# Decoder kernel, second cross attention: four engines issue in the order of the text instead of the scheduler's

## The chip, the cores and the metric

One core of a Trainium2 chip. The metric is the time of one execution in microseconds (us) of device time. The kernel before took 1747.34 us, median of three runs (1746.52, 1749.41, 1747.34). A profiled execution of it is used for everything below.

Engines by their names in the profile: PE is TensorE (matmul; PEld its weight loads), DVE is VectorE, ACT is ScalarE, POOL is GpSimd, SP is SyncE, which issues nearly all transfers. Each engine takes its own instructions strictly one after the other from its queue; semaphores order the engines among each other. L1361 means line 1361 of the kernel.

## The reference, cut to what matters

Two decoder layers over four sequences of 256 tokens, all in float32. The part that the change touches is the second layer's cross attention: 16 query heads in 4 groups that share keys and values, head size 128, and 256 + 1601 = 1857 keys for each sequence.

```python
q = (draft_hidden @ Wq.T).reshape(bsz, draft_len, H, HD)
q = _rms_norm(q, q_norm_w).transpose(0, 2, 1, 3)
kv_in = jnp.concatenate([context_hidden, draft_hidden], axis=1)
k = (kv_in @ Wk.T).reshape(bsz, total_len, KVH, HD)
v = (kv_in @ Wv.T).reshape(bsz, total_len, KVH, HD).transpose(0, 2, 1, 3)
k = _rms_norm(k, k_norm_w).transpose(0, 2, 1, 3)
q = _rope(q, draft_position_ids)
k = _rope(k, full_position_ids)
scores = jnp.einsum('bhqd,bhkd->bhqk', q, k) * SCALE
probs = jax.nn.softmax(scores, axis=-1)
attn = jnp.einsum('bhqk,bhkd->bhqd', probs, v)
return attn @ Wo.T
```

It is followed by a mixture of eight experts (`experts` in the kernel), which for one sequence is computed beside the attention of the next.

## The kernel before, in words

The kernel is written as generators that emit instructions, in a framework that records them, finds the dependencies, sets the semaphores, and lets a scheduler choose the order in which each engine gets its instructions. The first part (the first layer, and the recurrence of the second) fills about the first 500 us. The rest is `steps()` (L1531), started beside the end of the first part and then emptied by `run(work)` at L1596.

Work is done in 32 pairs of heads (4 sequences, 4 groups, 2 pairs in each). A pair has 256 tokens x 2 heads = 512 query columns and 15 tiles of 128 keys, the last of 65. Two key tiles make a chunk, so a pair has 8 chunks, the last with the 65 keys alone. One step `s` of the text emits, in this order:

- `exponential` (L1381) for the chunk scored ten steps earlier (`DE = 10`): DVE subtracts the row maximum from 128x1024 scores (L1383), ACT takes the exponential in place (L1386), POOL adds both halves to the sum (L1389 and L1398).
- `score` (L1349) for chunk `s`, twice: PE computes a 128x512 tile of scores `bsc` in PSUM in two passes (L1361); ACT copies it to SBUF with the key's norm as scale (L1362); DVE takes it into the running maximum `acc` (L1364 for the first tile of a pair, L1366 for the others).
- `others(2 s)`, then `weigh` (L1400) for the chunk of eleven steps earlier (`DW = 11`): PE multiplies the exponentials by the values into `bpo` (L1407, two tiles, four passes); then `others(2 s + 1)`.

`others` (L1524) emits what a table of places holds for that half step: `maximum` (L1368: four transposes `tm` on PE, a maximum `mq` on DVE, and a few half steps later four transposes `bc` that spread it), `finish` (L1409: `bpo` copied to `aT` on ACT, the sums `ts` turned by PE and DVE, and the output projection `bpw`, L1437, added to x on DVE, L1441), the queries of the next group (`prep_q`, L1229: `pq` on PE, squares L1189 on ACT, rotations L1190 and L1191 and a sum L1198 on DVE, an addition L1196 and a power L1199 on POOL that gives `rnq`, and later the scaling L1203 on ACT, transposes `tpq` and a copy to `qTb`), its keys in four pieces (`prep_kv`, L1258: the same with `pk`, then transposes `tpk` L1301 and the copy to `kTb` L1303), position angles and tables (L1115 to L1165), and the experts of the sequence before.

Score tiles and most other PSUM tiles go round six banks (`p1`). The scores wait in twelve SBUF chunks between `score` and `weigh`. Instructions that read the same PSUM tile on two engines are ordered by semaphores in the text's order: the copy L1362 is ahead of the maximum L1366 on the same tile, which waits for it.

The order on each engine's queue within this part was the scheduler's choice, as long as it kept the dependencies. The list `ENGINES` (L19) names PE, DVE, ACT and POOL.

The text of two of the functions named, for the order in one step:

```python
V.tensor_tensor(s[0:n, 0:w, :], s[0:n, 0:w, :], self.bc[0:n, None, :].to_broadcast([n, w, 512]), ALU.subtract)
A.activation(s[0:n, 0:w, :], s[0:n, 0:w, :], AF.Exp)
...
T.matmul(pc[0:n, :], lhsT=e["kT"][:, k * P : k * P + n], rhs=q, start=True, stop=True)
A.activation(s[0:n, i, :], pc[0:n, :], AF.Copy, scale=e["kn"][0:n, k : k + 1])
...
V.scalar_tensor_tensor(self.acc[0:n, :], pc[0:n, :], e["kn"][0:n, k : k + 1], self.acc[0:n, :], ALU.mult, ALU.max)
```

Of the kernel before, what the change touches and what calls it, by code (L numbers as in the profile page):

```python
# [12 lines left out]
ENGINES = (mybir.EngineType.PE, mybir.EngineType.DVE, mybir.EngineType.Activation, mybir.EngineType.Pool)  # L13
# [103 lines left out]
def decoder_kernel(ctx: ExitStack, tc: tile.TileContext, at, t, out):  # L117
# [988 lines left out]
    def run(gen):  # L1106
        for _ in gen:
            pass
# [422 lines left out]
    def steps():  # L1531
        for s in range(STEPS):
            n, c = divmod(s, NPAIR)
            m, i = divmod(s - DE, NPAIR)
            if 0 <= m < len(pairs):
                pairs[m].exponential(i)
            if n < len(pairs):
                pairs[n].score(c)
            others(2 * s)
            m, i = divmod(s - DW, NPAIR)  # L1540
            if 0 <= m < len(pairs):
                pairs[m].weigh(i)
            others(2 * s + 1)
            yield s
# [15 lines left out]
    work = steps()  # L1560
# [32 lines left out]
    run(late)  # L1593
    run(keys)
    run(first)
    run(work)  # L1596
    assert not places, sorted(places)
    gen = experts(B - 1)
    for _ in range(KEPT):
# [70 lines left out]
```

## Time and profile before

| | us |
|---|---|
| profiled execution | 1749.43 |
| its span, first to last instruction | 1747.4 |
| PE busy | 1694.9 (97%) |
| DVE busy | 1302.7 (75%) |
| ACT busy | 997.4 (57%) |
| POOL busy | 877.5 (50%) |

Busy time counts the time in which at least one instruction of an engine runs; instructions that follow each other overlap a little, so an instruction's own duration is longer than the distance to the next start. In the group rows the figures after the bar are busy time and mean nanoseconds of one instruction, and after the second bar the engine's idle time just ahead of them, with what ended most of it. In rows of the timeline: start, length, engine, line, operation, tiles, shapes, number of instructions merged into the row, and the idle time before it. In rows of waits: total us, how many, the longest.

### The profile page before, as it was taken

How to read it: one execution, taken by the hardware profiler on the slowest of the kernel's cores; microseconds unless marked ns; L12 is line 12 of the kernel's file. 1: busy time of each engine (PE TensorE's matmuls, PEld its weight loads, DVE VectorE, ACT ScalarE, POOL GpSimd, SP SyncE). 2: the span in 40 equal slices, each digit the busy share in tenths (PEclk: the TensorE clock that was granted, in tenths of full speed). 3: DMA queues.
4: the chain of work that ended last, by engine and by line, in shares of the span. 5: the costliest groups of instructions: out<-in, count | busy, mean ns of one | idle time of the engine just before them, and what ended most of it. 6: DMA issues, size and time to landing. Idle time of an engine off the chain costs nothing.

```text
span 1747.4 us, 20643 instructions
## 1 busy us (share of the span) xinstructions
PE 1694.9 (97%) x6642; PEld 971.5 (56%) x6642; DVE 1302.7 (75%) x2429; ACT 997.4 (57%) x1742; POOL 877.5 (50%) x719
## 2 busy tenths in 40 slices
PE   8899989999999999999999999999999999999998
PEld 4455668765555455554555555555555555445546
DVE  6653476787668777787877878777877878788776
ACT  3456653656456656566665656556565656656551
POOL 2210032211126576676766756655665776676651
PEclk9999999999999999999999999999999999999999
DMA  7221334212231121121212121121222113011102
GB/s 258 99 90 50 90 99 128 75 66 90 97 109 46 38 82 35 55 58 31 89 32 70 47 67 52 55 82 35 73 61 67 51 37 93 26 37 48 43 0 67
DMA packets 113554, 119.10 MB, mean 68 GB/s; under 512 B 10000, under 2 KB 87332, under 8 KB 113448
## 3 DMA queue, kind: packets, MB, share of 16 engines
q1 hardware_dynamic: 111624, 116.39, 21.6%
q10 hardware_dynamic: 1824, 1.41, 0.3%
q8 instruction: 53, 0.87, 0.2%
q14 instruction: 53, 0.43, 0.1%
HBM read 100.20 MB, written 17.57 MB: 67 GB/s over the span
## 4 chain that ended last, share of the span: by engine, by line
PE 64%; DVE 12%; POOL 9%; ACT 9%; issue 4%; DMA 1%; POOLq 0%; DVEq 0%; ACTq 0%
PE bpo L1407 17%; PE bsc L1361 16%; PE pk L1290 5%; POOL sum L1398 5%; PE mph L1053 2%; PE bpw L1437 2%; PE vah L355 2%; ACT s L1386 2%; ACT s L1362 2%; DVE acc L1366 1%; PE xpo L740 1%; DVE s L1383 1%; PE pq L1239 1%; POOL ropeq L1196 1%; PE xsc L695 1%
## 5 line engine op out<-in xcount | busy, mean ns | idle before, releaser
L1398 POOL TENSOR_TENSOR sum<-sum,s 128x512 f32<-128x512 f32 (+1 forms) x411 | 536.7, 1306 | 84.1 <-ACT s L1386 59.0
L1361 PE MATMUL bsc<-qTb,kTb 128*128 128x512 f32 (+1 forms) x960 | 459.5, 599 | 6.8 <-ACT kTb L1303 6.7
L1407 PE MATMUL bpo<-s,vb 128*128 128x512 f32 (+1 forms) x960 | 459.9, 598 | 0.4 <-ACT s L1386 0.4
L1362 ACT ACTIVATE s<-bsc,kn 128x512 f32<-128x512 f32 (+1 forms) x480 | 316.5, 683 | 211.6 <-PE bsc L1361 194.6
L1366 DVE SCALAR_TENSOR_TENSOR acc<-bsc,kn,acc 128x512 f32<-128x512 f32 x448 | 333.0, 743 | 89.2 <-ACT s L1362 73.3
L1383 DVE TENSOR_TENSOR s<-s,bc 128x1024 f32<-128x1024 f32 (+1 forms) x256 | 289.4, 1142 | 14.7 <-PE bc L1379 14.5
L1386 ACT ACTIVATE s<-s 128x1024 f32<-128x1024 f32 (+1 forms) x256 | 256.5, 1006 | 53.8 <-DVE s L1383 52.2
L1361 PEld LDWEIGHTS bsc<-qTb,kTb 128*128 128x128 f32 (+1 forms) x960 | 174.2, 188 | 191.9 <-issue 135.3
L1407 PEld LDWEIGHTS bpo<-s,vb 128*128 128x128 f32 (+1 forms) x960 | 169.8, 191 | 141.7 <-issue 137.9
L1389 POOL TENSOR_TENSOR sum<-s 128x512 f32<-128x512 f32 x32 | 40.8, 1276 | 198.6 <-ACT s L1386 198.6
L1196 POOL TENSOR_TENSOR ropek<-ropek,ropuk 128x512 f32<-128x512 f32 (+1 forms) x64 | 78.2, 1222 | 123.7 <-DVE ropuk L1191 122.4
L1203 ACT ACTIVATE ropeq<-ropeq,rnq 128x128 f32<-128x128 f32 x128 | 41.2, 390 | 110.7 <-POOL rnq L1199 107.1
L355 PE MATMUL vah<-wv,vcT 128*128 128x512 f32 (+1 forms) x156 | 77.7, 633 | 5.1 <-DMA vcT<-in_ctxT 3.1
L1290 PEld LDWEIGHTS pk<-wkv,cTk 128*128 128x128 f32 x624 | 76.3, 192 | 8.3 <-issue 4.5
L1290 PE MATMUL pk<-wkv,cTk 128*128 128x128 f32 x624 | 77.4, 275 | 0.0
L1199 POOL TENSOR_TENSOR kn<-ssk,nhalf 128x4 f32<-128x4 f32 (+1 forms) x64 | 66.2, 1034 | 17.5 <-DVE ssk L1198 15.0
L1364 DVE TENSOR_SCALAR acc<-bsc,kn 128x512 f32<-128x512 f32 x32 | 24.0, 750 | 59.7 <-ACT s L1362 59.7
L1437 PEld LDWEIGHTS bpw<-wo,aT 128*128 128x128 f32 x256 | 48.5, 190 | 34.8 <-issue 21.1
L272 POOL TENSOR_TENSOR rsr_xa<-rse_xa,nhalf 128x2 f32<-128x2 f32 x4 | 3.4, 854 | 126.0 <-DVE rse_xa L270 126.0
L1437 PE MATMUL bpw<-wo,aT 128*128 128x256 f32 x256 | 65.6, 379 | 0.3 <-ACT aT L1413 0.3
L1196 POOL TENSOR_TENSOR ropeq<-ropeq,ropuq 128x512 f32<-128x512 f32 x32 | 43.8, 1368 | 40.2 <-PE bsc L1361 17.8
L358 ACT COPY vst<-vah 128x512 f32<-128x512 f32 (+1 forms) x52 | 30.2, 591 | 56.0 <-issue 18.3
(509 smaller groups left out, 2589.7 us busy)
## 6 DMA issues: line engine op xcount, KB each, us to landing
v<-vst SPq DMA_DIRECT2D x48, 256.0 KB
vb<-v SPq DMA_DIRECT2D x48, 256.0 KB
cTk<-in_ctxT SPq DMA_DIRECT2D x24, 512.0 KB
wq<-in_wq SPq DMA_DIRECT2D x16, 512.0 KB
wo<-in_wo SPq DMA_DIRECT2D x16, 512.0 KB
wi<-in_wi SPq DMA_DIRECT2D x32, 256.0 KB
xcT<-in_ctxT SPq DMA_DIRECT2D x12, 512.0 KB
xct<-in_ctx SPq DMA_DIRECT2D x12, 512.0 KB
```

The costliest lines, as they stand in the source:

```text
L355: T.matmul(pv[0:r, :], lhsT=cT[:, c, k * P : k * P + r], rhs=wv[c], start=c == 0, stop=c == 1)
L1196: G.tensor_tensor(r4, r4, u4[:, :, ::-1, :], ALU.add)
L1199: G.tensor_tensor(rn, ss[:, 0:n], nhalf[:, 0:n], ALU.pow)
L1290: T.matmul(pk[:, q, 0:w], lhsT=src, rhs=e["wkv"][:, c, 0:w], start=c == 0, stop=c == 1)
L1361: T.matmul(pc[0:n, :], lhsT=e["kT"][:, k * P : k * P + n], rhs=q, start=True, stop=True)
L1362: A.activation(s[0:n, i, :], pc[0:n, :], AF.Copy, scale=e["kn"][0:n, k : k + 1])
L1366: V.scalar_tensor_tensor(self.acc[0:n, :], pc[0:n, :], e["kn"][0:n, k : k + 1], self.acc[0:n, :], ALU.mult, ALU.max)
L1383: V.tensor_tensor(s[0:n, 0:w, :], s[0:n, 0:w, :], self.bc[0:n, None, :].to_broadcast([n, w, 512]), ALU.subtract)
L1386: A.activation(s[0:n, 0:w, :], s[0:n, 0:w, :], AF.Exp)
L1398: G.tensor_tensor(self.sum[0:n, :], self.sum[0:n, :], s[0:n, i, :], ALU.add)
L1407: T.matmul(self.po, lhsT=e["v"][0:n, k, :], rhs=self.s[c][0:n, i, :], start=k == 0, stop=k == NCH - 1)
L1437: T.matmul(pw[:, j * 256 : j * 256 + 256], lhsT=aT[:, o : o + P], rhs=e["wo"][:, self.h + h, :], start=True, stop=True)
```

## The change

The call that empties `steps()` is put into a region of the framework. Within it each of the four engines gets its instructions in the order in which the text emits them; the order across engines, SP's order, and where the region stands among instructions outside it stay with the scheduler. Steps 0 to 6 are emitted before the region, and the last sequence's experts after it.

```diff
@@ -1593,7 +1593,8 @@
     run(late)
     run(keys)
     run(first)
-    run(work)
+    with tc.manual_schedule(engines=set(ENGINES)):
+        run(work)
     assert not places, sorted(places)
     gen = experts(B - 1)
     for _ in range(KEPT):
```

## The prediction

> **What bounds the kernel now.** I read the page first: the chain that ended last, then the costliest groups.
>
> ```profile
> PE 64%; DVE 12%; POOL 9%; ACT 9%; issue 4%; DMA 1%; POOLq 0%; DVEq 0%; ACTq 0%
> ...
> L1361 PE MATMUL bsc<-qTb,kTb 128*128 128x512 f32 (+1 forms) x960 | 459.5, 599 | 6.8 <-ACT kTb L1303 6.7
> L1407 PE MATMUL bpo<-s,vb 128*128 128x512 f32 (+1 forms) x960 | 459.9, 598 | 0.4 <-ACT s L1386 0.4
> L1362 ACT ACTIVATE s<-bsc,kn 128x512 f32<-128x512 f32 (+1 forms) x480 | 316.5, 683 | 211.6 <-PE bsc L1361 194.6
> L1366 DVE SCALAR_TENSOR_TENSOR acc<-bsc,kn,acc 128x512 f32<-128x512 f32 x448 | 333.0, 743 | 89.2 <-ACT s L1362 73.3
> ```
>
> Most of the chain is PE, and the other engines wait for it. Two scores of PE (L1361) feed two readers each: ACT's copy (L1362) and DVE's running maximum (L1366). The last row shows what the change will act on: DVE's maximum waits for ACT's copy, although both only read the same PSUM tile. The program's waits agree: each L1366 waits for ACT and, through acc, for the DVE instruction before it.
>
> Next the stage itself, from the first pair's last score to the last pair's (531.4 to 1684.7 us: 31 pairs of heads, 37.2 us each), and DVE's waits in it.
>
> ```profile
> core 0: us, PE busy (x) PEld busy (x) DVE busy (x) ACT busy (x) POOL busy (x), PEclk, DMA share, GB/s
> 531.40:1684.70 1153.30, 1133.75 (x4016) 612.31 (x4015) 922.68 (x1498) 698.48 (x1152) 764.40 (x614) 1.00 0.18 53
> ```
>
> ```profile
> DVE acc L1366 <- ACT s L1362: 68.8, 62, 4.3
> DVE acc L1364 <- ACT s L1362: 59.1, 26, 5.2
> ```
>
> PE is busy 98% of it. DVE is busy 922.7 us and stands 230.6. That is the room in which a worse order of DVE is free; past it, each microsecond of standing lengthens the kernel.
>
> **The change.** No instruction of the computation is added or removed. From step 7 on, four engines take the text's order. Comparing the two builds: PE's order hardly differs (a pass or two of L1407, or two scores, at each of the 15 head changes, and a little at both ends), DVE's goes backwards against the text at 355 places before and at none after, ACT's at 255, POOL's at 89. SP stays with the scheduler: some 11 of its 203 transfers change place (positions, rawk, wo, one we), with DMA 18% busy in the stage and a stage that gets longer around them; I take 0.
>
> The text of one step says, per engine: DVE subtracts (L1383, an old pair), then L1366, L1366, then whatever else; ACT takes the exponential (L1386) of that same subtraction, then copy, copy (L1362). Before, the scheduler issued subtractions ahead of the maxima, 8.7 places early on average. Now a circle closes in every step: subtraction, exponential behind it, copy behind the exponential, maximum behind the copy, next step's subtraction behind the maxima. DVE stands while ACT takes the exponential and the first copy, and nothing of its queue may pass. Behind it in that queue are both maxima, which free PSUM, and the rotations of the next keys; PE waits for those, with a step in hand.
>
> The price of one round, from rows of the timeline (DVE, then ACT, then a pair of maxima in a row):
>
> ```profile
> 881.92 0.75 DVE L1366 SCALAR_TENSOR_TENSOR acc<-bsc,kn,acc 128x512 f32<-128x512 f32 x1 [4.24 <-ACT s L1362]
> ...
> 883.90 1.19 DVE L1383 TENSOR_TENSOR s<-s,bc 128x1024 f32<-128x1024 f32 x1
> 885.00 0.75 DVE L1366 SCALAR_TENSOR_TENSOR acc<-bsc,kn,acc 128x512 f32<-128x512 f32 x1
> 885.67 1.21 DVE L1383 TENSOR_TENSOR s<-s,bc 128x1024 f32<-128x1024 f32 x1
> ```
>
> ```profile
> 880.28 1.04 ACT L1386 ACTIVATE s<-s 128x1024 f32<-128x1024 f32 x1
> 881.22 1.24 ACT L1362 ACTIVATE s<-bsc,kn 128x512 f32<-128x512 f32 x2
> ...
> 885.12 1.06 ACT L1386 ACTIVATE s<-s 128x1024 f32<-128x1024 f32 x1 [0.25 <-DVE s L1383]
> ```
>
> ```profile
> 889.46 1.61 DVE L1366 SCALAR_TENSOR_TENSOR acc<-bsc,kn,acc 128x512 f32<-128x512 f32 x2 [0.54 <-issue]
> ```
>
> Subtraction 1.20; the exponential starts 0.03 after its end (885.09 to 885.12); the copy starts 0.94 after the exponential (880.28 to 881.22) and takes 0.67; the maximum starts 0.03 after the copy's end (881.89 to 881.92); the second starts 0.86 after the first (1.61 less 0.75), for it needs acc; the next instruction follows 0.67 later. Sum 4.40. The same three DVE instructions in a row cost 1.11 + 0.67 + 0.67 = 2.45 (starts at 883.90, 885.00, 885.67). So a full step adds 1.95 us of standing. Of eight steps, one subtracts 65 rows (0.68 for 1.20, an exponential of 0.53 for 0.94): 3.47 against 1.92, adds 1.55. One scores 65 rows, once: 3.54 against 1.78, adds 1.76. A pair: 6 x 1.95 + 1.55 + 1.76 = 15.0 us.
>
> All other DVE work (rotations L1190/L1191, L1198, mq, updates of x, experts, tables) stands in the text after the second maximum and before the next subtraction: it lies beside ACT's copies, not in the standing time, so it adds in full. In the stage DVE is then busy 922.7, stands 15.0 x 30.75 = 461 (steps 10 to 255, where a score and an exponential meet), and gets some 7 us of angle rows (L1131 to L1140) that the scheduler had put ahead of 531. ACT's table loads (1.28 each) with three activations of 1.0 to 1.1 stand between a copy and an exponential at three places; some 2.4 us of each overhang: 7. Sum 1398 for 1153.3: +244. What DVE must wait for besides is there a step early: PE needs only the exponential of the step before, and its work (some 4.6 us a step by the spacing of its starts, all else included) is under the new 5.6 (1398 over 248 steps).
>
> What improves is then covered. ACT waits 104.3 us for POOL's rnq (L1203 from L1199), and PE stands four times some 2.4 us behind that or its like (at 751.8, 1059.8, 1374.7, 1547.4); text order puts L1203 behind the copies. And at head changes PE loses its filler: tpk at 857.23, a pass of L1407 at 857.66, kTb copied from 857.87, the score at 858.53; without the pass 0.87 us x 15 = 13 us. Both lie beside the DVE circle and cost or bring nothing while it binds; if that cover is gone they are the rival below. The tail after 1684.7 has no scores: unchanged, 0 (between -3 and +5).
>
> Outside the stage nothing is taken: 1747.4 + 244 = 1991, and the profiled execution lasted 2.0 us more than its span (1749.43), 2.1 above the median. I take 1994. Low end: other DVE work counted as 922.7 less all busy time of L1383, L1366 and L1364 (280.5 + 322.5 + 23.3) is 296, though their rows overlap their neighbours by 0.07 to 0.09; with the circle's bare 33.4 a pair (8 x 4.40 less 0.93 and 0.86) over 30.75 pairs this gives 1027 + 296 + 14 for the stage, 1933 in all. High end: PE standing long enough to lose its clock, below, in part: +60, 2055.
>
> A rule beside this: PE's clock. After PE stood 2.26, 2.45 and 2.34 us (751.84, 1059.79, 1547.38) the granted clock was 0.5 for 3.41 us; after 2.15 us (1374.70) it was not. [...] By the row a step with rotations of keys (4.4 + 1.9 against PE's 4.3) comes near it, one to three a pair: up to 5 us of a pair's 8 us spare. [...]
>
> **Rivals.** A, PE remains the bound: the standing fits into DVE's 230.6 us because maxima need not follow copies, or ACT is further ahead than the text says. It decides where a pair's circle with its other work stays below 37.2 us; I get 45. For it: PE's 98%, and PE's order all but unchanged. Against: the two rows of DVE waiting for ACT. Time: the four stands (9.2), kTb late for the fourth chunk (some 7) and late expert rows (3) go, 13 come: 6 less, 1743 against the execution's 1749.43, faster than before. 5%.
>
> B, PE's half clock feeds back: longer stands, slower PE, so that PE sets the pace. One half-clock window a step costs 8 x 1.7 on 36.7 us of work (PE's passes at their back-to-back spacing, 1137 us for 31 pairs), 50.3 a pair: 31 x 13.1 more, 2155. For it: stands near 2.2 us in steps with keys. Against: a slower PE stands less. 8%.
>
> C, half of the other DVE work slips into the standing time (about 120 us less), as where the exponential is ready early: 1870. Against: the built order has nothing between subtraction and maximum. That the order is not taken at all, I exclude: it is in the build. 5%.
>
> **How the numbers follow.** Forecast 82%, A 5, B 8, C 5. Its own range is 1933 to 2055; 1925 to 2075 leaves out A, B and C and little else. A measurement of this kernel tells about 0.2% (3.5 us) from no change: faster 0.04 (most of A), same 0.02, slower 0.94.
>
> **What would show it.** DVE's waits L1366 <- ACT s L1362 grow from 62 to over 400, some 1.7 us each; ACT's exponential waits for DVE's subtraction in nearly every step; L1383 and L1386 alternate step by step; pairs of 44 to 46 us; PE busy near 80%; L1203 no longer waits for rnq. It is wrong if DVE's maxima run while an exponential of the same step is still on ACT, or if PE stays over 95% busy.

## The result, and the profile after

The changed kernel takes 2008.22 us, median of four runs (2007.57 to 2012.01), against 1747.90 us (1746.52 to 1749.41) for the kernel before on the same chip: a ratio of 1.1494, 95% interval [1.1474, 1.1514]. The predicted 1994 lies 14 us below it. The profiled execution lasted 2007.57 us, its span 2005.8. All further rows of the changed kernel are of that execution.

The chain that ended last, and the four groups that were shown of before, now read on the page of the changed kernel:

```profile
PE 36%; DVE 34%; ACT 15%; issue 12%; DMA 1%; POOL 1%; DVEq 0%; ACTq 0%; SPq 0%; POOLq 0%
...
L1366 DVE SCALAR_TENSOR_TENSOR acc<-bsc,kn,acc 128x512 f32<-128x512 f32 x448 | 336.0, 750 | 391.5 <-ACT s L1362 366.7
...
L1361 PE MATMUL bsc<-qTb,kTb 128*128 128x512 f32 (+1 forms) x960 | 485.9, 626 | 115.4 <-ACT kTb L1303 99.9
L1407 PE MATMUL bpo<-s,vb 128*128 128x512 f32 (+1 forms) x960 | 475.5, 616 | 37.3 <-ACT s L1386 30.4
...
L1362 ACT ACTIVATE s<-bsc,kn 128x512 f32<-128x512 f32 (+1 forms) x480 | 301.5, 673 | 7.3 <-PE bsc L1361 7.2
```

The chain went from 64% PE to 36% PE, 34% DVE and 15% ACT. The instructions themselves hardly change on DVE and ACT (mean 750 ns for 743, 673 for 683). What is new is the idle time of DVE's maximum behind ACT's copy: 366.7 us for 73.3. ACT's copy, in turn, no longer waits for PE: 7.2 us for 194.6. PE has become the engine that is ahead.

The waits of the changed kernel:

```profile
ACT s L1386 <- DVE s L1383: 678.5, 246, 5.4
...
DVE acc L1366 <- ACT s L1362: 366.7, 219, 4.8
...
PE bsc L1361 <- ACT kTb L1303: 99.9, 49, 4.6
...
DVE acc L1364 <- ACT s L1362: 51.6, 31, 1.7
```

Before, the first of these rows read:

```profile
ACT s L1386 <- DVE s L1383: 52.2, 68, 2.6
```

246 of 256 exponentials wait for their subtraction, where 68 did, and the two kinds of maximum together wait 250 times, once in nearly every one of the 256 steps that score. 366.7 + 51.6 = 418.3 us over 250 is 1.67 us each.

One whole turn of the circle, from the timeline of the changed kernel, DVE first, then ACT over the same time:

```profile
1018.41 1.21 DVE L1383 TENSOR_TENSOR s<-s,bc 128x1024 f32<-128x1024 f32 x1
1021.32 1.61 DVE L1366 SCALAR_TENSOR_TENSOR acc<-bsc,kn,acc 128x512 f32<-128x512 f32 x2 [1.70 <-ACT s L1362]
1022.84 0.41 DVE L1059 SCALAR_TENSOR_TENSOR it<-it,mph 128x256 f32<-128x256 f32 x1
1023.29 0.42 DVE L1060 TENSOR_TENSOR it<-it,mph 128x256 f32<-128x256 f32 x1
1023.62 1.22 DVE L1383 TENSOR_TENSOR s<-s,bc 128x1024 f32<-128x1024 f32 x1
```

```profile
1019.65 1.06 ACT L1386 ACTIVATE s<-s 128x1024 f32<-128x1024 f32 x1 [4.37 <-DVE s L1383]
1020.61 1.25 ACT L1362 ACTIVATE s<-bsc,kn 128x512 f32<-128x512 f32 x2
```

Subtraction, exponential, copy, maxima, subtraction: 1023.62 - 1018.41 = 5.21 us, of which two expert rows take 0.78 (1022.84 to 1023.62). 4.43 remain, where 4.40 were predicted. This turn is no exception: each of the stage's 244 subtractions is followed on DVE by a maximum at once, and the idle time between the two is 1.70 us in the median, and nearly everywhere (1.27 where 65 rows are subtracted). The reader is to see two things: that DVE has nothing to do between 1019.62 and 1021.32, and that ACT has nothing before 1019.65. Each engine is idle while the other works.

By stretches of time (from the first pair's last score to the last pair's, and the rest):

```profile
core 0: us, PE busy (x) PEld busy (x) DVE busy (x) ACT busy (x) POOL busy (x), PEclk, DMA share, GB/s
528.60:1928.80 1400.20, 1200.34 (x4016) 624.35 (x4015) 943.54 (x1505) 685.67 (x1151) 749.24 (x611) 0.96 0.14 43
1928.80:2005.80 77.00, 61.65 (x243) 40.41 (x241) 45.97 (x107) 20.49 (x32) 22.25 (x18) 0.96 0.12 38
```

The stage lasts 1400.2 us (1153.3 before; 1398 predicted), 45.2 a pair. DVE stands 1400.2 - 943.5 = 456.7 us in it (230.6 before). The tail lasts 77.0 us, where 62.7 were left unchanged in the prediction: that is nearly the whole miss. The same row of the kernel before:

```profile
1684.70:1747.40 62.70, 56.89 (x243) 39.67 (x241) 41.86 (x99) 15.88 (x26) 17.80 (x14) 1.00 0.15 46
```

### The profile page after: what moved, and what is told of

The parts are those of the page before. It is cut to its first block, busy times and chain, and to the rows that moved or that the text cites. A ratio compares the mean times of both kernels' runs of the same rounds, so it can differ in the third digit from the quotient of the medians.

```text
span 2005.8 us, 20665 instructions
## 1 busy us (share of the span) xinstructions
PE 1765.7 (88%) x6642; PEld 984.1 (49%) x6642; DVE 1321.1 (66%) x2429; ACT 985.1 (49%) x1743; POOL 865.3 (43%) x719
## 4 chain that ended last, share of the span: by engine, by line
PE 36%; DVE 34%; ACT 15%; issue 12%; DMA 1%; POOL 1%; DVEq 0%; ACTq 0%; SPq 0%; POOLq 0%
DVE s L1383 10%; DVE acc L1366 10%; ACT s L1362 9%; PE bsc L1361 6%; PE bpo L1407 5%; PE vah L355 3%; PE pq L1239 2%; DVE x L1441 1%; DVE ropuk L1191 1%; PE mph L1053 1%; PE pp L822 1%; PE pk L1290 1%; PE xpo L740 1%; PE xsc L695 1%; DVE ssk L1198 1%
## 5 line engine op out<-in xcount | busy, mean ns | idle before, releaser
L1398 POOL TENSOR_TENSOR sum<-sum,s 128x512 f32<-128x512 f32 (+1 forms) x411 | 529.3, 1288 | 455.6 <-ACT s L1386 422.0
L1366 DVE SCALAR_TENSOR_TENSOR acc<-bsc,kn,acc 128x512 f32<-128x512 f32 x448 | 336.0, 750 | 391.5 <-ACT s L1362 366.7
L1361 PE MATMUL bsc<-qTb,kTb 128*128 128x512 f32 (+1 forms) x960 | 485.9, 626 | 115.4 <-ACT kTb L1303 99.9
L1407 PE MATMUL bpo<-s,vb 128*128 128x512 f32 (+1 forms) x960 | 475.5, 616 | 37.3 <-ACT s L1386 30.4
L1362 ACT ACTIVATE s<-bsc,kn 128x512 f32<-128x512 f32 (+1 forms) x480 | 301.5, 673 | 7.3 <-PE bsc L1361 7.2
L1407 PEld LDWEIGHTS bpo<-s,vb 128*128 128x128 f32 (+1 forms) x960 | 174.2, 197 | 197.4 <-issue 133.5
L1389 POOL TENSOR_TENSOR sum<-s 128x512 f32<-128x512 f32 x32 | 40.7, 1273 | 71.7 <-ACT s L1386 71.7
L1199 POOL TENSOR_TENSOR kn<-ssk,nhalf 128x4 f32<-128x4 f32 (+1 forms) x64 | 63.5, 992 | 17.4 <-DVE ssk L1198 14.8
L1053 PE MATMUL mph<-yTm,wi 128*128 128x256 f32 x256 | 61.8, 386 | 0.0
L1239 PE MATMUL pq<-wq,yTb 128*128 128x512 f32 x128 | 60.3, 593 | 0.0
L1441 DVE SCALAR_TENSOR_TENSOR x<-bpw,rs,x 128x256 f32<-128x256 f32 x128 | 55.3, 472 | 5.3 <-PE bpw L1437 5.3
L1364 DVE TENSOR_SCALAR acc<-bsc,kn 128x512 f32<-128x512 f32 x32 | 24.0, 751 | 51.6 <-ACT s L1362 51.6
```

Source lines behind the costliest of these rows:

```text
L1239: T.matmul(pq, lhsT=d["yT"][:, c, j * P : (j + 1) * P], rhs=e["wq"][:, c, :], start=c == 0, stop=c == 1)
L1398: G.tensor_tensor(self.sum[0:n, :], self.sum[0:n, :], s[0:n, i, :], ALU.add)
L1407: T.matmul(self.po, lhsT=e["v"][0:n, k, :], rhs=self.s[c][0:n, i, :], start=k == 0, stop=k == NCH - 1)
```

## The experiments

Theory: the loss is the circle of DVE and ACT, closed because both take the text's order. Rivals: PE's order (the filler gone at the head changes), one of the two queues alone, and a collapse of PE's clock. (On the last: the granted clock is 0.5 for 99 us of the stage, which can cost PE at most about half of that, an estimate, while PE stands 1400.2 - 1200.3 = 199.9 us besides. It does not set the pace.) All times below are medians with the kernel before timed on the same chip (1747.22, 1749.54 and 1746.34 us for the three groups of runs), and ratios are to that.

### Which engines' order

Six kernels differ from the changed one in the list of engines alone:

```diff
-    with tc.manual_schedule(engines=set(ENGINES)):
+    with tc.manual_schedule(engines={mybir.EngineType.PE}):                                     # e1
+    with tc.manual_schedule(engines={mybir.EngineType.DVE}):                                    # e2
+    with tc.manual_schedule(engines={mybir.EngineType.Activation}):                             # e3
+    with tc.manual_schedule(engines={mybir.EngineType.DVE, mybir.EngineType.Activation}):       # e4
+    with tc.manual_schedule(engines={mybir.EngineType.Activation, mybir.EngineType.Pool}):      # e10
+    with tc.manual_schedule(engines={mybir.EngineType.Activation, mybir.EngineType.PE}):        # e11
```

PE alone:

> Only TensorE takes the text's order; VectorE, ACT and POOL stay with the scheduler. Theory (the circle subtraction, exponential, copy, maximum makes the loss): the circle is not there, since the scheduler still puts subtractions ahead. What is left is the filler lost at 15 head changes, 0.87 us each: 1748 to 1765 us. Rival (TensorE's order makes the loss, its waits for kTb are 99.9 us of the changed kernel): at least 1840.

VectorE alone:

> Only VectorE takes the text's order. Theory: the circle needs both queues, and on ACT the scheduler now puts a step's copies ahead of its exponential, so the maxima find their copies done: 1745 to 1800 us. Rival (text order on VectorE alone makes the loss, because its subtractions come late): 1950 to 2010.

ScalarE alone:

> Only ACT takes the text's order. Theory: VectorE's subtractions still run ahead, so an exponential seldom waits and the circle is open: 1740 to 1800 us. Rival (ACT's order alone makes the loss, copies held up behind exponentials): 1950 to 2010.

VectorE and ScalarE:

> VectorE and ACT take the text's order, TensorE and POOL stay with the scheduler, which can fill TensorE's waits as it likes. Theory: the whole circle is there: 1985 to 2015 us, some 1.7 us of VectorE standing in each of about 219 steps. Rival (TensorE's order and its waits for kTb carry a good part of the loss): below 1930.

ACT with one of the two engines that are not in the circle:

> ACT and POOL in text order, PE and DVE left to the scheduler. ACT alone gave 1733.0. POOL's queue has the sums of the exponentials and the rotations' sums for the norm rnq; on no run so far does a row show that POOL's order binds. Theory (only a circle of two engines that both take the text's order costs much, and it takes DVE and ACT): POOL's order is covered, 1728 to 1742. Rival: POOL closes a second circle with ACT, since the sum waits for the exponential and ACT's scaling of the queries waits for rnq behind that sum: 1745 to 1775, and the wait of L1203 for rnq is back.

> ACT and PE in text order, DVE and POOL left to the scheduler. PE alone cost 14 us (the filler at the head changes is gone), ACT alone gained 14 us. Theory 1, the two are separate and add: 1744 to 1752. Theory 2, ACT's order already gives the key copies early enough that PE needs no filler: 1729 to 1739. Rival of both, ACT and PE close a circle of their own through copy, PSUM bank and score: over 1765.

| text order on | us | ratio, 95% interval |
|---|---|---|
| PE (e1) | 1762.03 | 1.0082 [1.0066, 1.0097] |
| DVE (e2) | 1766.33 | 1.0107 [1.0090, 1.0125] |
| ACT (e3) | 1732.96 | 0.9913 [0.9899, 0.9928] |
| DVE and ACT (e4) | 1997.66 | 1.1428 [1.1411, 1.1445] |
| ACT and POOL (e10) | 1729.86 | 0.9892 [0.9873, 0.9911] |
| ACT and PE (e11) | 1744.56 | 0.9985 [0.9976, 0.9994] |

DVE alone costs 19 us, ACT alone brings 14, and the two together cost 250. That is no sum of two prices: the loss needs both, as a circle does. The waits of the run with both:

```profile
ACT s L1386 <- DVE s L1383: 678.5, 247, 6.7
...
DVE acc L1366 <- ACT s L1362: 367.2, 219, 4.9
...
PE bpo L1407 <- ACT s L1386: 143.1, 100, 4.2
...
PE bsc L1361 <- ACT kTb L1303: 4.3, 9, 0.5
```

The first two rows are those of the changed kernel to within 0.5 us. PE's waits are quite others (its order is the scheduler's here): it stands 143 us for exponentials and 4 for keys, instead of 30 and 100. The time hardly notices, 1998 for 2008: PE's and POOL's text order add at most some 10 of the 260 us to what DVE's and ACT's make. So PE's stands in the changed kernel lie nearly all beside the circle, as the prediction had them.

With one of the two queues left free, the circle is open. With ACT's order free (e2), ACT copies ahead of the exponential: in one step of its timeline two copies start at 1002.59, the subtraction on DVE at 1003.13, the maxima at 1004.26 without a wait, and the exponential only at 1004.62. With DVE's order free (e3), the subtraction has been issued ahead, and ACT waits for subtractions in 39 places (102.6 us), not 246.

e3 came out below its range, and below the kernel before. Two rows of ACT's waits, first of the kernel before, then of e3, say what went:

```profile
ACT ropeq L1203 <- POOL rnq L1199: 107.1, 31, 6.5
```

```profile
ACT ropeq L1203 <- POOL rnq L1199: 3.6, 5, 1.6
```

The scheduler had put the scaling of the queries (L1203) where ACT stood for a norm still under way on POOL; the text has it behind the copies. In the stage PE's idle time falls from 19.6 us (1153.30 - 1133.75) to 6.1 (1132.60 - 1126.53), its busy time by 7.2 more, and the mean granted clock of the run is 0.996, where it was 0.993. This is the gain that the prediction priced inside rival A (19 us, of which 9 for these stands) and held to be covered.

PE's text order costs 15 us alone (e1), and 12.5 on top of ACT's (e11 is 1.8 below its own runs of before, e3 14.3): close to the 13 that rows of one head change gave. e11 fits the theory of two separate prices. In e10 the further gain over e3 (ratio 0.9892 for 0.9913) is inside the intervals, so POOL's order is worth nothing that these runs can tell; e3 and e10 both beat the kernel before and the changed one. e10's 1729.86 us is the lowest median of all these kernels; against the kernel before it is a gain of 1.1%.

### Opening the circle at one point

The maximum ahead of the copy, for the changed kernel (e5) and for the kernel before (e8):

```diff
-                A.activation(s[0:n, i, :], pc[0:n, :], AF.Copy, scale=e["kn"][0:n, k : k + 1])
                 if k == 0:
                     V.tensor_scalar(self.acc, pc, e["kn"][:, 0:1], None, ALU.mult)
                 else:
                     V.scalar_tensor_tensor(self.acc[0:n, :], pc[0:n, :], e["kn"][0:n, k : k + 1], self.acc[0:n, :], ALU.mult, ALU.max)
+                A.activation(s[0:n, i, :], pc[0:n, :], AF.Copy, scale=e["kn"][0:n, k : k + 1])
```

> Text order on all four engines, but score() emits VectorE's maximum ahead of ACT's copy of the same tile, so that the copy waits for the maximum and VectorE waits for TensorE alone. Theory: the circle is cut, VectorE's standing falls from 457 us of the stage to below 250, TensorE binds again: 1740 to 1785 us. Rival (text order costs on all engines, in many small waits): 1900 or more.

> The kernel before with VectorE's maximum emitted ahead of ACT's copy of the same tile, order left to the scheduler on all engines: tells what the swap is worth without the text order. Theory: TensorE binds, as before; VectorE waits less for ACT, ACT more for VectorE: 1735 to 1765 us. If the swap itself, and not the cut circle, brought the gain of the run with text order, this one would gain by a similar amount, to about 1500 to 1600.

Measured: 1825.07 us (1.0440 [1.0418, 1.0462]) and 1794.89 (1.0260 [1.0245, 1.0275]). Both missed upwards. The direction of e5 is right: turning one edge of the circle (one hand-over between the engines) round takes 185 of the 260 us away (75.5 above before are left), with all four engines in text order. But the edge costs something of its own. In e8, in the scheduler's order, it costs 45 us. Two of its waits (the copy is L1366 there, the maxima L1363 and L1365):

```profile
ACT s L1366 <- DVE acc L1365: 166.6, 125, 3.4
...
PE bsc L1361 <- ACT s L1366: 35.5, 16, 4.0
```

Now ACT waits for DVE's maxima, and PE for the banks that ACT then frees late. That is about half of the 45 us: in the stage PE stands 44.4 us for 19.6 before. For the other half PE is busy 20.0 us longer, at a mean granted clock of 0.981 in the run for 0.993 before.

In e5 DVE's standing in the stage did fall below 250 us, to 1221.2 - 979.5 = 241.7, but PE did not become the bound again: it stands 1221.2 - 1149.6 = 71.6 us, with 49.5 us of waits for keys in the whole run, and ACT's exponentials still wait for subtractions in 217 places. In e5 other waits come up that the circle had covered; two rows of its waits:

```profile
DVE ropek L1190 <- ACT squares L1189: 66.4, 55, 6.0
...
DVE ropeq L1190 <- ACT squares L1189: 60.6, 31, 3.6
```

In the changed kernel the same two rows are 8.0 us (11 times) and 13.0 (16). DVE's rotations need ACT's squares; while DVE stood at its maxima, ACT had the time to make them. Which of these waits sets e5's time is not shown.

The exponential later, all four engines in text order (e6), and with ACT alone in text order (e12): a new method takes the exponential and POOL's sums out of `exponential`, and is called one step after the subtraction.

```diff
                 s[0:n, 0:w, :], s[0:n, 0:w, :], self.bc[0:n, None, :].to_broadcast([n, w, 512]), ALU.subtract
             )
+
+        def power(self, c):
+            n, w, s = self.rows[c], self.wide[c], self.s[c]
             A.activation(s[0:n, 0:w, :], s[0:n, 0:w, :], AF.Exp)
...
                 pairs[m].exponential(i)
+            m, i = divmod(s - DW, NPAIR)
+            if 0 <= m < len(pairs):
+                pairs[m].power(i)
             if n < len(pairs):
                 pairs[n].score(c)
             others(2 * s)
-            m, i = divmod(s - DW, NPAIR)
```

> Text order on all four engines, but ACT's exponential and POOL's sums of a chunk are emitted one step after its subtraction (ahead of that step's scores), so no exponential waits for a subtraction of its own step. Theory: the circle is cut at another place; copies no longer wait for a fresh subtraction: 1740 to 1800 us, with some waits of the value products for the exponential of their own step. Rival (the maximum's wait for the copy is the cost, wherever the exponential stands): above 1900.

> ACT alone in text order, with the exponential and POOL's sums emitted one step after its subtraction. ACT's waits for the subtraction (102.6 us in 39 places with ACT alone) should nearly vanish. Theory: PE is the bound in that kernel (it stands for almost nothing), so nothing or little is gained: 1728 to 1737. Rival 1: a good part of ACT's waits still reaches PE: 1715 to 1728. Rival 2: the exponential comes so near its use that PE waits for it, as in the run with all four engines (25 us): 1740 to 1765.

e6 took 1773.00 us (1.0139 [1.0121, 1.0157]): 237 of the 260 us are gone (23.5 above before are left), with every instruction of all four engines still in an order written in the text. Its waits (the exponential is L1389 there):

```profile
DVE acc L1366 <- ACT s L1362: 62.2, 90, 5.0
...
ACT s L1389 <- DVE s L1383: 49.6, 37, 3.8
...
PE bpo L1410 <- ACT s L1389: 25.2, 21, 3.0
```

Both edges of the circle have fallen to the size that they had before the change (73.3 and 52.2 us). The last row is the largest new wait of PE (0.4 us before), as the expectation named it. PE's standing in the stage is 1175.1 - 1138.5 = 36.6 us for 19.6, which is most of the 23.5 us that are left. ACT has an exponential to take whose subtraction lies a whole step back. This is the plainest evidence for the theory: most of the loss is not the price of a fixed order, but of one distance in it.

e12 took 1741.12 us (0.9966 [0.9953, 0.9979]), slower than ACT's text order without the shift. That is the lower edge of the rival in which the exponential comes too near its use, but the row named for it is small (PE waits 3.2 us for exponentials in four places, and 7.3 for keys in 14). A new row of its waits is that of copies behind POOL's sums, which moved with the exponential and hold the score chunk a step longer:

```profile
ACT s L1362 <- POOL sum L1401: 60.5, 37, 4.7
```

Which of these makes the 9 us (5.2 below before, for e3's 14.3) is open.

The exponential behind the scores of its step (e7):

```diff
             m, i = divmod(s - DE, NPAIR)
-            if 0 <= m < len(pairs):
-                pairs[m].exponential(i)
             if n < len(pairs):
                 pairs[n].score(c)
+            if 0 <= m < len(pairs):
+                pairs[m].exponential(i)
             others(2 * s)
```

> Text order on all four engines, but a step emits its two scores ahead of its subtraction and exponential. The circle stays (subtraction, exponential, next step's copy, next step's maximum), but the other VectorE work now lies inside the standing time. Theory: a step lasts 4.40 us where the other work is under 1.76 us and 2.64 us plus that work elsewhere: a mean near 4.8 us, 1760 to 1840 us. Rival (the circle is not what binds): no difference from the changed kernel, 1990 to 2020.

A miss: 2027.81 us (1.1588 [1.1551, 1.1625]), slower than the changed kernel. The expectation was that DVE would now do its rotations and expert updates while ACT takes the exponential. The timeline of this kernel, DVE and then ACT:

```profile
1008.80 1.21 DVE L1383 TENSOR_TENSOR s<-s,bc 128x1024 f32<-128x1024 f32 x1
1011.41 0.42 DVE L1190 TENSOR_TENSOR ropek<-pk,ctabk 128x256 f32<-128x256 f32 x1 [1.40 <-ACT squares L1189]
```

```profile
1010.05 1.06 ACT L1386 ACTIVATE s<-s 128x1024 f32<-128x1024 f32 x1 [2.22 <-DVE s L1383]
1011.01 0.37 ACT L1189 ACTIVATE squares<-pk 128x256 f32<-128x256 f32 x1
```

The work that was to fill the gap waits itself for ACT: the rotation reads the tile that ACT squares, and the squares now stand behind the exponential, which waits for the subtraction. The circle was moved one place round, not opened: DVE's maxima still wait 267.9 us for copies, and its rotations and expert rows 66.7 + 60.7 + 38.1 = 165.5 us for ACT, where it was 8.0 + 13.0 + 8.7 in the changed kernel. In all DVE stands 1419.6 - 951.4 = 468.2 us in the stage, 11.5 more than in the changed kernel.

### The tail

The one stretch that was priced wrong. All four engines in text order while the text scores, the last sixteen steps free:

```diff
     with tc.manual_schedule(engines=set(ENGINES)):
-        run(work)
+        while step < NPAIR * len(pairs):
+            step = next(work) + 1
+    run(work)
```

> All four engines in text order only as long as the text still scores (up to step 255); the last sixteen steps, which hold no scores, go back to the scheduler. It tests the one stretch that my sum priced at nothing and that came out 14.3 us longer (77.0 for 62.7 us after the last score). Theory: the order of these last steps costs it, because the exponentials, the copies of bpo and the sums stand in a line where PE needs them (stands of 1.5, 2.1, 0.6, 1.3 and 0.8 us of PE are shown there): then 1993 to 1999. Rival: it is what the circle leaves undone at the last score, DVE's and ACT's backlog, which no order of the tail can give back (the stand of 3.8 us for the last maximum and the half clock behind it): then 2004 to 2010. The stage before 1929 should stay at 1400 in both.

Measured: 2002.18 us (2000.09 to 2004.52), between the two ranges, and the windows say why. The tail's row in e9:

```profile
1932.30:1999.00 66.70, 57.50 (x243) 39.51 (x241) 46.30 (x104) 20.53 (x32) 22.19 (x17) 1.00 0.14 44
```

The tail takes 66.7 us, against 77.0 in the changed kernel and 62.7 before. The stage is 3.0 us longer in this execution (1403.2). So in these profiles the order of the tail was worth 10.3 of the 14.3 us, and 4.0 were left. PE in the changed kernel's tail, then in e9's:

```profile
1938.01 0.94 PE L1373 MATMUL tm<-cst,acc 128*128 128x128 f32 x4 [3.81 <-DVE acc L1366]
1938.75 5.04 PE L1407 MATMUL bpo<-s,vb 128*128 128x512 f32 x8
...
1947.18 2.53 PE L1407 MATMUL bpo<-s,vb 128*128 128x512 f32 x4 [2.08 <-ACT aT L1413]
...
1958.79 3.70 PE L1407 MATMUL bpo<-s,vb 128*128 128x512 f32 x8 [0.61 <-ACT s L1386]
1963.82 1.99 PE L1407 MATMUL bpo<-s,vb 128*128 128x512 f32 x4 [1.33 <-ACT s L1386]
1966.59 1.12 PE L1407 MATMUL bpo<-s,vb 65*128 65x512 f32 x2 [0.78 <-ACT s L1386]
```

```profile
1938.92 1.98 PE L1407 MATMUL bpo<-s,vb 128*128 128x512 f32 x4 [2.45 <-ACT s L1386]
...
1945.72 0.43 PE L1421 MATMUL ts<-sum,cst 128*32 128x128 f32 x8 [1.36 <-POOL sum L1398]
1946.08 1.56 PE L1437 MATMUL bpw<-wo,aT 128*128 128x256 f32 x6
1947.48 7.03 PE L1407 MATMUL bpo<-s,vb 128*128 128x512 f32 x16
1954.34 0.59 PE L1437 MATMUL bpw<-wo,aT 128*128 128x256 f32 x2
1954.77 6.17 PE L1407 MATMUL bpo<-s,vb 128*128 128x512 f32 x14
```

In text order PE takes the last pairs' weighing in nine pieces and stands before five of them (four are shown), for exponentials or for the copy `aT`; the stand of 3.81 us is also followed by a lower clock (a granted 0.5 for 3.41 us from 1938.24 on: eight passes take 5.04 us at 1938.75, where eight took 3.60 in the tail of before). Left to the scheduler, it runs 16 and 14 passes at a stretch. Two stands of e9 are not in the tail of before, 2.45 + 1.36 = 3.8 us, for an exponential and a sum: that is the size of the 4.0 that no order of the tail gave back, work that the stage had left late, the rival's part.

## Why the prediction was right, step by step

- The circle was right, place and price: 4.43 us a turn for 4.40, 1.70 us of it idle between subtraction and maximum where the prediction's chain gives 0.03 + 0.94 + 0.67 + 0.03 = 1.67. It needs DVE's and ACT's queues together (e2, e3 and e4) and falls when one distance in it is changed (e6).
- The stage was right in sum, 1400.2 for 1398, and that the sum came so near is in part luck. DVE was to be busy 922.7 + 7 = 930 and to stand 461 + 7 = 468; it was busy 943.5 and stood 456.7. Of the 456.7, 411.6 lie between a subtraction and its maximum and 23.9 between the two maxima of a step; the other 21.2, most of them rotations that wait, were priced at nothing. Against that, the 1.95 us a step were not all standing: 0.09 at the subtraction and 0.08 at the second maximum are rows that no longer overlap their neighbour, which is busy time, by the prediction's figures some 40 us. Busy time grew by only 20.9, 7 of them the angle rows, for before the change a good many rows stood alone already: the overlap of neighbouring rows in the stage fell from 96.0 us (in 1190 places) to 73.3 (in 905). The two errors are of 20 to 30 us each, and they cancel.
- The table loads were right: the three maxima behind them wait 4.85, 3.68 and 3.39 us where a turn has 1.70, an overhang of 6.8 us for the 7 taken.
- That DVE's other work lies beside ACT's copies, and not in the standing time, held: rival C's half did not slip in. All 244 subtractions of the stage have the maximum next behind them on DVE.
- "What DVE must wait for besides is there a step early" held for DVE (rotations wait 21.0 us in all for squares) but only because DVE stood elsewhere: e5 and e7, which were to give it that time, made the same rows 127 us in either kernel. In the prediction's sum it is a part of the 21.2 us above. In e7 it is what the expectation had wrong; in e5 it is one of the waits that came up.
- For PE it did not hold at the head changes. Keys come late there, 99.9 us in 49 places for 6.7 in ten, because the copy to `kTb` stands behind an exponential that waits for its subtraction. e4 shows that this lies beside the circle, but for 10 us at most.
- The head change without filler was priced at 13 us and hidden; laid bare it was 14.8 (e1) and 12.5 (e11 against e3). The gain of text order on ACT was priced at 19 and hidden; laid bare it was 14.3 (e3). Rival A would have been 6 us faster than before; its like, e11, is 1.8 faster.
- PE's clock: 24 half-clock stretches in the stage, some 0.8 a pair, and two in the tail. The prediction's row gave one to three a pair. The stretches did not set the stage's time, as said. PE was busy 86% of the stage, not near 80%: work at half clock counts as busy (all 3.41 us of the stretch from 569.50 on are), and 99 us of the stage at half clock for 10 before make up to some 44 (an estimate) of the 67 us by which PE's busy time grew; the rest is open.
- The step that failed is the tail, "unchanged, 0 (between -3 and +5)", which measured +14.3. The tail has no scores, so no circle; but it has the last pairs' subtractions and exponentials in a line, and PE's weighing in text order behind them. It is the mis-sized term: 10.3 us of it are order and 4.0 the stage's backlog (e9). With the stage's start 2.8 us earlier and its length 2.2 us over, the three add to 13.7, nearly all of the 14.2 by which the prediction was short. (1994 is the sum for a profiled execution, and that one lasted 13.6 longer. The 2.1 us by which the profiled execution of before lay above its median was named and not taken off.)
- The count of waits, "over 400", was wrong in form only: the second maximum of a step follows the first, so there is one wait a step, 250 in all, of the size named.

## What to carry to other kernels

In this kernel fixing the order of one queue cost 19 us at most or was even a gain; fixing two that hand work to each other twice within a step closed a circle, whose length is the sum of its instructions and hand-overs. Before such a fix, walk once round the step across the engines and ask for each edge whether its producer is a whole step back: moving one exponential, with the sums behind it, a step later was worth 237 us here. And when a large wait is removed, the smaller waits of the same engine that it had covered come up; look for who feeds the work that is to fill the gap.

## What the runs showed of the hardware

In the changed kernel PE's granted clock is 0.5 in 26 stretches between 526 us and PE's last instruction: 22 of 3.41 us, three of 6.83 and one of 10.24. The stands of PE just ahead of them, or at their beginning, are 1.88 to 4.58 us long. The length of a stand did not decide it alone: PE stood 1.88 us up to 1589.22, and the clock was 0.5 from 1590.08 on; it stood 3.40 us up to 1014.99, and the clock was 1.00 all the way from 1004 to 1035. So the prediction's four stands, with half clock after 2.26 us and none after 2.15, give no limit that holds in the changed kernel. What decided besides the length is not shown.
